# A Mamba layer's prologue: x and the gate in one tile with one Silu, the convolution's bias added at the PSUM read

## The chip, the cores and the metric

The kernel runs on one core of a Trainium2 chip. A core has a matrix engine (TensorE, PE in the profile; its weight loads are PEld), VectorE (DVE), ScalarE (ACT), GpSimd (POOL), and SyncE (SP), which here issues the DMAs. They work in parallel, each through its own list of instructions in a fixed order, and wait for one another by semaphores. The metric is the device time of one execution in microseconds (us).

## The reference

Eight layers follow one another on an activation of 8 sequences of 256 positions and 128 channels. The change is in the seventh, a pair of Mamba scans (one forward, one on the reversed sequence) between layernorms. One scan computes:

```python
xz = x @ W_in.T
xp, z = jnp.split(xz, 2, axis=-1)
xc = conv_general_dilated(xp, conv_w, ..., feature_group_count=E)   # 4 taps, causal
xc = _silu(xc + conv_b)
x_dbl = xc @ W_xp.T
dt_lo, Bm, Cm = (x_dbl[..., :R], x_dbl[..., R:R + N], x_dbl[..., R + N:])
dt = softplus(dt_lo @ W_dt.T + dt_b)
A = -jnp.exp(A_log)
def step(h, inp):                         # one position
    dA = jnp.exp(dtt[:, :, None] * A)
    h = dA * h + (dtt * xt)[:, :, None] * Bt[:, None, :]
    y = jnp.einsum('ben,bn->be', h, Ct)
y = ys + xc * Dp
y = y * _silu(z)
return y @ W_out.T
```

E is 256 channels, N is 64 states, R is 8. What matters here: x passes through a convolution, a bias and a Silu and then feeds everything that follows; the gate z passes through a Silu too, but is used only at the very end.

## The kernel before

The first six layers are interleaved by a planner of their own and end before the part that matters. The Mamba layer (`l3_attn`, from line 1838) works in eight units. A unit is two sequences (512 positions) in one direction: unit u has the pair u // 2, forward for even u and reversed for odd u. Channels lie on the partitions, so x, the gate and dt are tiles of 128 partitions by 2 by 512.

Each unit has three parts.

`prologue` (lines 1902 to 1991) makes what the scan needs. For an even unit it first normalizes x (two runs of `norm_steps` and two products on POOL). It transposes x, and copies it to `xT` (L1921). For each of two channel blocks and two sequences, four matmuls (L1929) make the convolution in PSUM, and ScalarE copies 128x256 of it to `xc` (L1931). Two matmuls (L1936) make the gate, copied to `sz` (L1938). Then come the Silus on ScalarE: two of 128x512 with the convolution's bias on `xc` (L1941), one of 128x1024 on `sz` (L1942). From `xc`, L1947 and L1950 make C, dt's low-rank part and B, copied at L1953 and L1954 and sent by SP to DRAM (`cd`) and turned (`Bt`). L1962 makes dt's argument; softplus is made of ScalarE's Abs (L1965), Exp (L1967) and four Squares (L1972) with VectorE's L1966, L1974 and L1975. POOL makes `dtx` (L1978), PE transposes it, ScalarE copies it to `dtxT` (L1990).

The loop runs 64 steps a unit, one for each state n. `start` (L2047) has SP fetch C's row to all partitions (`Cs`), ScalarE make dA by two Exps of 128x512 (L2058), and for even n scale `dtxT` by B four times (`sT`, L2055). `inputs` fills the PSUM tile `ps_h` by transposes of `sT` for even n (L2073), or by 64x64 matmuls with `dB` for odd n (L2071; `dB` is made on POOL at L2045). `scan` runs VectorE's scan over 1024 elements (L2079) and the product with C (L2081) on POOL, for one n of sixteen on VectorE. `add` transposes that into the PSUM accumulator `ps_y` (L2091).

`epilogue` (lines 1993 to 2038) turns `ps_y` back, adds xc times D on VectorE (L2006), multiplies by `sz` on POOL (L2008), projects (L2014), and after each odd unit adds both directions, normalizes twice and adds to the residual (L2022 to L2038).

The order of the work is written by hand: prologue and epilogue are generators, and each step of the loop advances each by one `yield`. The prologue of unit u + 1 starts at step 6 of unit u and has to end by step 60; the epilogue of unit u - 1 runs in the first steps of unit u. Prologue 0 runs alone ahead of the loop. After that a scheduler puts each engine's instructions into their final order, by when it takes their inputs to be ready, so the order in the trace isn't always the order of the source: the first of L1941's two Silus runs as soon as its half of `xc` is there, before the other half is copied.

The names to know: the PSUM tiles of the prologue and the epilogue (`ps_a`) and of the loop (`ps_h`) share one ring of three buffers. `dA`, `sT` and `h` have three buffers each, `xc`, `sz`, `dt`, `dtxT` two. Silu and Exp live in different activation tables, so ScalarE loads a table (ACT_TABLE_LOAD, put down to the line of the instruction that needs it) when it goes from one to the other; copies, Identity, Abs and Square run without one here.

Of the kernel before, what the change touches and what calls it, by code (L numbers as in the profile page):

```python
# [8 lines left out]
F32 = mybir.dt.float32  # L9
BF16 = mybir.dt.bfloat16  # L10
I32 = mybir.dt.int32
AF = mybir.ActivationFunctionType
# [4 lines left out]
P = 128  # L17
NB = 8
L = 256
# [247 lines left out]
def over(ap, n, axis):  # L267

    a = ap.unsqueeze(axis)
    s = list(a.shape)  # L270
    s[axis] = n
    return a.to_broadcast(s)
# [1565 lines left out]
def l3_attn(k):  # L1838
# [13 lines left out]
    nc = k.nc  # L1852
    U = 2 * L
    N = 64
    HALF = (slice(0, 64), slice(64, 128))
    with ExitStack() as es:
        s1 = es.enter_context(k.tc.tile_pool(name="l3a_s1", bufs=1))
        s2 = es.enter_context(k.tc.tile_pool(name="l3a_s2", bufs=2))
# [5 lines left out]
        def pb(name="ps_a"):  # L1864
            return psum.tile([P, 2, U], F32, name=name, tag="b")
# [25 lines left out]
        def by_seq(t):  # L1891
            return t.rearrange("p (b t) -> p b t", t=L)

        def turned(name, src):

            t = s2.tile(list(src.shape), F32, name=name)
            for b in range(2):
                for j in range(2):
                    nc.sync.dma_start(out=t[HALF[b], j::2], in_=src[HALF[j], 2 * b:2 * b + 2])
            return t  # L1900

        def prologue(u, o):
            g, m = divmod(u, 2)
            w = k.l3a[m]
            if m == 0:
                xs = xns[g] = s2.tile([P, 4, D], F32, name="xn")
                yield from k.norm_steps(xs, k.x[:, 4 * g:4 * g + 4, :], 4)
                yield from k.norm_steps(xs, xs, 4)
                nc.gpsimd.tensor_tensor(xs, xs, over(k.l3a_ln[:, 0, :], 4, 1), ALU.mult)
                nc.gpsimd.tensor_tensor(xs, xs, over(k.l3a_ln[:, 1, :], 4, 1), ALU.add)  # L1910
                yield
            xT, CL = xTs[u % 2], CLs[u % 2]
            ps = pb()
            for j in range(4):
                d = slice(j * P, (j + 1) * P)
                if m == 0:
                    nc.tensor.transpose(ps[:, 0, d], xns[g][:, j, :], k.ident)
                else:
                    nc.tensor.matmul(ps[:, 0, d], xns[g][:, j ^ 1, :], k.flip, start=True, stop=True)
            yield  # L1920
            nc.scalar.copy(xT[:, :, 3:3 + L], by_seq(ps[:, 0, :]))  # L1921
            yield

            xc, sz = s2.tile([P, 2, U], F32, name="xc"), s2.tile([P, 2, U], F32, name="sz")
            for ec in range(2):
                for b in range(2):
                    ps = pb()
                    for tap in range(4):
                        nc.tensor.matmul(ps[:, 0, 0:L], w["wk"][:, tap, ec * P:(ec + 1) * P], xT[:, b, tap:tap + L], start=tap == 0, stop=tap == 3)  # L1929
                    yield  # L1930
                    nc.scalar.copy(xc[:, ec, b * L:(b + 1) * L], ps[:, 0, 0:L])  # L1931
                    yield
                    yield
            for ec in range(2):
                ps = pb()
                nc.tensor.matmul(ps[:, 0, :], w["win"][:, 256 + ec * P:256 + (ec + 1) * P], xT[:, :, 3:3 + L], start=True, stop=True)  # L1936
                yield
                nc.scalar.copy(sz[:, ec, :], ps[:, 0, :])  # L1938
            yield
            for ec in range(2):  # L1940
                nc.scalar.activation(xc[:, ec, :], xc[:, ec, :], AF.Silu, bias=w["cols"][:, ec, 0:1])  # L1941
            nc.scalar.activation(sz, sz, AF.Silu)  # L1942
            yield

            ps = pb()
            for ec in range(2):
                nc.tensor.matmul(ps[0:72, 0, :], w["wxp"][:, ec, 64:136], xc[:, ec, :], start=ec == 0, stop=ec == 1)  # L1947
            for j in range(4):
                for ec in range(2):
                    nc.tensor.matmul(ps[:, 1, j * 64:(j + 1) * 64], xc[:, ec, j * P:(j + 1) * P], w["wxp"][:, ec, 0:64], start=ec == 0, stop=ec == 1)  # L1950
            yield
            B = s2.tile([P, 4, N], F32, name="B")
            nc.scalar.copy(CL[0:72, :], ps[0:72, 0, :])  # L1953
            nc.scalar.copy(B.rearrange("p j n -> p (j n)"), ps[:, 1, 0:256])  # L1954
            cd = dram.tile([N, U], F32, name="cd")
            nc.sync.dma_start(out=cd, in_=CL[0:64, :])
            Bt = turned("Bt", B)
            yield

            ps = pb()  # L1960
            for ec in range(2):
                nc.tensor.matmul(ps[:, ec, :], w["wdt"][64:73, ec * P:(ec + 1) * P], CL[64:73, :], start=True, stop=True)  # L1962
            un, zr = s2.tile([P, 2, U], F32, name="sp_u"), s1.tile([P, 2, U], F32, name="sp_z")
            yield
            nc.scalar.activation(un, ps, AF.Abs)  # L1965
            nc.vector.tensor_scalar(zr, ps, 0.0, None, ALU.max)  # L1966
            nc.scalar.activation(un, un, AF.Exp, scale=-1.0)  # L1967
            yield
            dt = s2.tile([P, 2, U], F32, name="dt")
            for j, (_, b) in enumerate(SP_FACTORS):  # L1970
                ps = pb()
                nc.scalar.activation(ps, un, AF.Square, bias=sp[:, j:j + 1])  # L1972
                yield
                nc.vector.scalar_tensor_tensor(dt, ps, b, dt if j else un, ALU.add, ALU.mult)  # L1974
            nc.vector.scalar_tensor_tensor(dt, dt, SP_LEAD, zr, ALU.mult, ALU.add)  # L1975
            yield
            dtx = s1.tile([P, 2, U], F32, name="dtx")
            nc.gpsimd.tensor_tensor(dtx, dt, xc, ALU.mult)  # L1978

            nc.gpsimd.memset(dt.rearrange("p e (b t) -> p e b t", t=L)[:, :, :, 0:1], 1e23)  # L1980
            yield
            yield
            dtxT = s2.tile([P, 4, 2, P], F32, name="dtxT")
            ps = pb()
            for j in range(4):
                for ec in range(2):
                    n = 2 * j + ec
                    nc.tensor.transpose(ps[:, n // 4, n % 4 * P:(n % 4 + 1) * P], dtx[:, ec, j * P:(j + 1) * P], k.ident)
            yield
            nc.scalar.copy(dtxT.rearrange("p (a j) e c -> p a (j e c)", a=2), ps)  # L1990
            o.update(xc=xc, sz=sz, cd=cd, dt=dt, dtxT=dtxT, dtxTt=turned("dtxTt", dtxT), B=B, Bt=Bt)
# [106 lines left out]
        for _ in prologue(0, made[0]):  # L2098
            pass
# [4 lines left out]
        for i in range(units * N + 4):  # L2104
            u, n = divmod(i, N)
            if n == N - 4:
                for _ in ahead:
                    pass
            if i + 3 < units * N:
                pre(made[(i + 3) // N], (i + 3) % N)  # L2110
            v, c = divmod(i - 1, N)
            if 1 <= i <= units * N:
                inputs(made[v], sts[i - 1], c)
            if i < units * N:
                sts[i] = start(made[u], k.l3a[u % 2], n)
                if n == 6 and u + 1 < units:
                    ahead = prologue(u + 1, made[u + 1])
            if 1 <= i <= units * N:
                scan(sts[i - 1], c)
            if i >= 4:  # L2120
                v, c = divmod(i - 4, N)
                add(made[v], sts.pop(i - 4), c)
                if c == N - 1:
                    for _ in behind:
                        pass
                    behind = epilogue(v, made[v])
            next(behind, None)
            next(ahead, None)
# [115 lines left out]
```

## Time and profile before

| what | value |
|---|---|
| time, median of 3 runs | 4469.94 us (4467.84 to 4470.97) |
| the profiled execution: time, span | 4469.94 us, 4468.1 us |
| granted TensorE clock | 0.922 of full speed |
| busy over the span: PE, DVE, ACT, POOL | 82%, 67%, 58%, 61% |
| prologue 0 | about 2886 to 2931 us |
| loop of the Mamba layer, first to last scan | 2937 to 4380 us |
| last layer | to 4468 us |

The whole span's shares say little of the Mamba loop, which takes a third of the time. There all engines are much busier: from 2930 to 4110 us POOL is busy for 1058.87 of 1180 us, ACT for 1019.72, DVE for 1000.43 and PE for 980.42. The chain that the page follows back from the end covers only the last layer. So the loop has to be read from stretches of it and from what each engine waited for. A line of the groups gives busy time in all and the mean of one instruction in ns, then the engine's idle time just before them and what ended it. A line of the stretches gives busy us and number of instructions for each engine.

### The profile page before, as it was taken

The page shows a single profiled execution, that of the slowest core. Times are in us where ns is not written, and L with a number is a line of the kernel's source. Part 1 is how long each engine was busy: PE and PEld are TensorE (multiplying, and loading weights), DVE is VectorE, ACT ScalarE, POOL GpSimd, SP SyncE. Part 2 cuts the span into 40 slices and gives each one's busy share as a digit, 9 for nine tenths or more (in the row PEclk, how much of TensorE's full clock was granted, in tenths as well). Part 3 has the DMA queues.
Part 4 walks back from the last instruction along what each step waited for, and adds up shares of the span by engine and source line. Part 5 has one row for each costly group of instructions (what it writes and reads, how often), then busy time and mean ns, then how long its engine had stood idle before and what let it go on. Part 6 is the DMA issues. An engine that isn't in the chain of part 4 may idle for free. (4 is left out here: it accounts for less than half of the span.)

```text
span 4468.1 us, 125288 instructions
## 1 busy us (share of the span) xinstructions
PE 3674.6 (82%) x55265; PEld 2890.7 (65%) x55265; DVE 2972.4 (67%) x4237; ACT 2583.0 (58%) x4536; POOL 2722.2 (61%) x2023
## 2 busy tenths in 40 slices
PE   6887887888778888889988887678887987888886
PEld 4776776766666655555555555467776876777774
DVE  6566565666555555644374457669888987987995
ACT  4444444434444454445554434388978888898883
POOL 5556656555664534532133243569988987988993
PEclk8998998989899999999999799889989999999997
DMA  1000000000000100000000000023333332332330
GB/s 54 3 2 2 3 2 2 3 2 8 2 2 17 35 1 7 6 23 20 1 1 1 6 1 1 10 84 105 99 90 94 107 98 82 106 101 87 106 110 29
DMA packets 98678, 168.90 MB, mean 38 GB/s; under 512 B 16699, under 2 KB 26582, under 8 KB 98006
## 3 DMA queue, kind: packets, MB, share of 16 engines
q1 hardware_dynamic: 98134, 160.89, 12.0%
q8 instruction: 434, 7.11, 0.6%
q14 instruction: 110, 0.90, 0.1%
HBM read 153.51 MB, written 2.10 MB: 35 GB/s over the span
## 5 line engine op out<-in xcount | busy, mean ns | idle before, releaser
L2081 POOL TENSOR_TENSOR hc<-h,Cs 128x1024 f32<-128x1024 f32 x480 | 1127.7, 2377 | 123.1 <-DVE h L2079 114.6
L2079 DVE TENSOR_TENSOR_SCAN h<-dA,ps_h 128x1024 f32<-128x1024 f32 x480 | 1069.7, 2271 | 122.6 <-PE ps_h L2073 38.9
L2058 ACT ACTIVATE dA<-dt,A 128x512 f32<-128x512 f32 x1024 | 684.6, 714 | 176.4 <-DVE h L2079 151.1
L2091 PE MATMUL ps_y<-w_c_ident,hc 128*128 128x128 f32 x4096 | 569.5, 284 | 131.9 <-POOL hc L2081 103.2
L2091 PEld LDWEIGHTS ps_y<-w_c_ident,hc 128*128 128x128 f32 x4096 | 462.5, 144 | 185.3 <-POOL hc L2081 175.9
L2055 ACT ACTIVATE sT<-dtxT,B 128x256 f32<-128x256 f32 x1024 | 451.3, 495 | 4.3 <-PE ps_h L2073 4.3
L580 DVE SCALAR_TENSOR_TENSOR acc<-ps,w_l0a_conv,acc 128x254 f32<-128x254 f32 (+2 forms) x768 | 313.9, 473 | 56.2 <-ACT acc L574 55.9
L2071 PE MATMUL ps_h<-dB,dtxTt 64*64 64x64 f32 x16384 | 305.6, 225 | 44.8 <-DVE h L2079 34.3
L2071 PEld LDWEIGHTS ps_h<-dB,dtxTt 64*64 64x64 f32 x16384 | 270.1, 138 | 99.1 <-DVE h L2079 46.1
L2073 PE MATMUL ps_h<-w_c_ident,sT 128*128 128x128 f32 x2048 | 280.2, 282 | 61.3 <-DVE h L2079 35.8
L2073 PEld LDWEIGHTS ps_h<-w_c_ident,sT 128*128 128x128 f32 x2048 | 241.5, 146 | 79.0 <-DVE h L2079 32.9
L790 PE MATMUL ps<-Z,XY 64*64 64x64 f32 x4608 | 192.2, 242 | 86.4 <-DVE Z L774 80.4
L349 ACT COPY XY<-ps 128x1024 f32<-128x1024 f32 (+1 forms) x128 | 120.5, 945 | 238.6 <-PE ps L797 229.0
L732 POOL TENSOR_TENSOR Ps<-M,w_c_levels 128x512 f32<-128x512 f32 x192 | 241.1, 1272 | 24.5 <-DVE M L706 24.0
L790 PEld LDWEIGHTS ps<-Z,XY 64*64 64x64 f32 x4608 | 159.8, 152 | 107.7 <-DVE Z L774 69.6
L220 POOL TENSOR_SCALAR ln_rs<-ln_mv 128x4 f32<-128x4 f32 (+1 forms) x84 | 20.2, 242 | 285.7 <-DVE ln_mv L218 275.9
L797 PE MATMUL ps<-XY,Z 64*64 64x64 f32 x5120 | 191.3, 240 | 0.5 <-issue 0.5
L771 PE MATMUL ps<-XY,Ps 64*64 64x64 f32 x5120 | 119.7, 236 | 80.9 <-ACT XY L349 29.1
L797 PEld LDWEIGHTS ps<-XY,Z 64*64 64x64 f32 x5120 | 168.0, 152 | 0.8 <-issue 0.6
L771 PEld LDWEIGHTS ps<-XY,Ps 64*64 64x64 f32 x5120 | 101.6, 146 | 102.9 <-issue 56.3
L774 DVE TENSOR_TENSOR Z<-ps,w_c_ident 128x512 f32<-128x512 f32 x160 | 107.7, 684 | 84.2 <-PE ps L771 83.6
L341 PE MATMUL ps<-ident 128*128 128x512 bf16 x401 | 111.0, 428 | 61.5 <-DVE qn L1067 19.3
(459 smaller groups left out, 8649.4 us busy)
## 6 DMA issues: line engine op xcount, KB each, us to landing
Cs<-cd SPq DMA_DIRECT2D x512, 256.0 KB, 3.2
dtxTt<-dtxT SPq DMA_DIRECT2D x32, 128.0 KB, 3.8
wk<-in_l0a_w SPq DMA_DIRECT2D x8, 256.0 KB, 6.2
w_h<-in_l1f_h SPq DMA_DIRECT2D x4, 512.0 KB, 3.9
w_l2a<-in_l2a_w SPq DMA_DIRECT2D x3, 512.0 KB, 4.0
w_l0a_wg<-in_l0a_wg SPq DMA_DIRECT2D x1, 1024.0 KB
w_qk<-in_l0f_wqkv SPq DMA_DIRECT2D x2, 512.0 KB, 3.6
cv<-in_l3a_m_conv SPq DMA_DIRECT2D x2, 512.0 KB, 5.0
```

Of the source, the lines that this page charges most:

```text
L580: nc.vector.scalar_tensor_tensor(acc[:, n, s:L], p4[:, n, 0:L - s], conv[:, h2, 4 * j + n, 3 - s:4 - s], acc[:, n, s:L], ALU.mult, ALU.add,)
L732: nc.gpsimd.tensor_tensor(t, M[:, :, 0:64], over(k.l0a_levels[:, n, :], 8, 1), ALU.mult)
L771: nc.tensor.matmul(ps[to, a, at(j)], Ps[own, h, :], XY[own, t, at(i)], start=True, stop=True)
L790: nc.tensor.matmul(ps[own, a, at(j)], XY[rows, t, at(i)], Z[rows, za, at(zj)], start=True, stop=True)
L797: nc.tensor.matmul(ps[to, a, at(4 + j)], Z[rows, za, at(zj)], XY[rows, t, at(i)], start=True, stop=True)
L2055: nc.scalar.mul(st["s"][:, j], o["dtxT"][:, j], o["B"][:, j, n:n + 1])
L2058: nc.scalar.activation(dA[:, :, ec, :], by_seq(o["dt"][:, ec, :]), AF.Exp, scale=w["A"][:, ec, n:n + 1])
L2071: nc.tensor.matmul(ps[q, b, ec, j * 64:(j + 1) * 64], o["dtxTt"][rows, j, ec, q], dB[rows, j, :], start=True, stop=True)
L2073: nc.tensor.transpose(ps[:, j // 2, ec, j % 2 * P:(j % 2 + 1) * P], st["s"][:, j, ec, :], k.ident)
L2079: nc.vector.tensor_tensor_scan(h.rearrange(flat), st["dA"].rearrange(flat), st["in"].rearrange(flat), 0.0, ALU.mult, ALU.add)
L2081: (nc.vector if on_v else nc.gpsimd).tensor_tensor(st["hc"], h, over(by_seq(st["C"]), 2, 2), ALU.mult)
L2091: nc.tensor.matmul(o["py"][:, 2 * b + j, ec, :], st["hc"][:, b, ec, j * P:(j + 1) * P], k.ident, start=first, stop=n == N - 1, is_transpos ...
```

## The change

x's convolution and the gate now lie in one tile `xz` of 128 by 4 by 512; `xc` and `sz` are views of its halves. The convolution's bias is added when its PSUM is read, by an Identity with a bias column in place of the copy. One Silu of 128x2048 takes the place of the three.

```diff
-            xc, sz = s2.tile([P, 2, U], F32, name="xc"), s2.tile([P, 2, U], F32, name="sz")
+            xz = s2.tile([P, 4, U], F32, name="xz")
+            xc, sz = xz[:, 0:2, :], xz[:, 2:4, :]
             for ec in range(2):
                 for b in range(2):
...
-                    nc.scalar.copy(xc[:, ec, b * L:(b + 1) * L], ps[:, 0, 0:L])
+                    nc.scalar.activation(xc[:, ec, b * L:(b + 1) * L], ps[:, 0, 0:L], AF.Identity, bias=w["cols"][:, ec, 0:1])
...
-            for ec in range(2):
-                nc.scalar.activation(xc[:, ec, :], xc[:, ec, :], AF.Silu, bias=w["cols"][:, ec, 0:1])
-            nc.scalar.activation(sz, sz, AF.Silu)
+            nc.scalar.activation(xz, xz, AF.Silu)
             yield
```

## The prediction

> **What bounds the kernel now.** I read the page's costliest groups first, then the busy time by stretches, then ScalarE's instructions by form, then the timelines of single engines in one prologue. From the page, two engines carry the Mamba loop almost evenly:
>
> ```profile
> L2081 POOL TENSOR_TENSOR hc<-h,Cs 128x1024 f32<-128x1024 f32 x480 | 1127.7, 2377 | 123.1 <-DVE h L2079 114.6
> L2079 DVE TENSOR_TENSOR_SCAN h<-dA,ps_h 128x1024 f32<-128x1024 f32 x480 | 1069.7, 2271 | 122.6 <-PE ps_h L2073 38.9
> ```
>
> POOL's product at 2.38 us a step is the longest, DVE's scan at 2.27 us is close behind. POOL's 123 us of idle time nearly all ends with a scan, so where POOL is late it is because DVE was. Which engine is full where is seen in stretches of the loop (an ordinary one last):
>
> ```profile
> core 0: us, PE busy (x) PEld busy (x) DVE busy (x) ACT busy (x) POOL busy (x), PEclk, DMA share, GB/s
> 2968.00:3018.00 50.00, 45.04 (x762) 38.15 (x760) 39.78 (x20) 49.75 (x85) 41.99 (x21) 0.97 0.31 100
> 3178.00:3227.00 49.00, 43.20 (x761) 36.68 (x759) 37.29 (x18) 48.38 (x83) 40.79 (x20) 1.00 0.33 104
> 3347.00:3384.00 37.00, 31.91 (x545) 25.48 (x543) 26.71 (x22) 34.49 (x64) 30.25 (x17) 0.95 0.31 91
> ...
> 3067.00:3106.00 39.00, 32.92 (x704) 28.93 (x704) 36.84 (x17) 34.02 (x64) 38.82 (x20) 1.00 0.36 109
> ```
>
> In the ordinary stretch POOL is full (38.82 of 39 us). In the first three, while the next unit's prologue runs, ScalarE is full (49.75 of 50, 48.38 of 49) and POOL and DVE lose 7 to 12 us each. So for some 50 us of each unit ScalarE is the bound. What it does there besides the loop's own work:
>
> ```profile
> L2058 ACT ACT_TABLE_LOAD x21 | 26.9, 1283 | 0.2
> L1941 ACT ACT_TABLE_LOAD x15 | 19.2, 1283 | 0.3
> L1941 ACT ACTIVATE xc<-xc,w_l3a_m_cols 128x512 f32<-128x512 f32 x16 | 11.6, 724 | 0.2
> L1931 ACT COPY xc<-ps_a 128x256 f32<-128x256 f32 x32 | 11.4, 355 | 5.9 <-PE ps_a L1929 5.8
> ...
> L1942 ACT ACT_TABLE_LOAD x7 | 9.0, 1283 | 0.1
> L1942 ACT ACTIVATE sz<-sz 128x1024 f32<-128x1024 f32 x8 | 8.5, 1058 | 0.1
> ```
>
> 22 loads stand ahead of a Silu and 21 ahead of the next dA: three Silus a unit run at three different times, each between Exps. One such excursion in ScalarE's timeline, and what DVE waited for in the same prologue (unit 2's); columns are start, duration, what ran, and in brackets the idle time before it and what ended it:
>
> ```profile
> 3195.62 1.28 ACT L1941 ACT_TABLE_LOAD   x1
> 3196.91 0.72 ACT L1941 ACTIVATE xc<-xc,w_l3a_m_cols 128x512 f32<-128x512 f32 x1
> 3197.66 1.28 ACT L2058 ACT_TABLE_LOAD   x1
> 3198.95 1.34 ACT L2058 ACTIVATE dA<-dt,A 128x512 f32<-128x512 f32 x2
> ```
>
> ```profile
> 3205.07 6.64 DVE L2079 TENSOR_TENSOR_SCAN h<-dA,ps_h 128x1024 f32<-128x1024 f32 x3 [2.14 <-PE ps_h L2073]
> 3214.38 4.46 DVE L2079 TENSOR_TENSOR_SCAN h<-dA,ps_h 128x1024 f32<-128x1024 f32 x2 [2.66 <-ACT dA L2058]
> 3224.11 1.23 DVE L1966 TENSOR_SCALAR sp_z<-ps_a 128x1024 f32<-128x1024 f32 x1 [5.26 <-ACT sp_u L1965]
> ```
>
> The first of these waits is ScalarE's too: the matmul it names (L2073) sat 1.48 us for the copy of sz (L1938), which held one of three PSUM buffers. With 0.94 us more at 3186.25 DVE lost 11.0 us in this prologue behind ScalarE.
>
> **What the Trainium skill says.** "ScalarE: Activation LUTs", section "What ACT_TABLE_LOAD costs", prices a load at about 1283 ns and the drain beside it at about 1380 ns more. The trace agrees on the load (1283) and shows no drain here: the excursion above runs from 3195.62 to 3198.95, 3.33 us, and 1.28 + 0.72 + 1.28 is 3.28. The same page, section "Table sets: the hidden batching unit", asks for calls to be batched by set; the 43 loads above are what it costs not to. The first section also gives an ACTIVATE as a fixed part and 0.833 ns an element; from this trace's Silus of 128x1024 at 1058 ns, 128x2048 is then an estimated 1058 + 853 = 1911 ns. "PSUM — Partial Sum Buffer", section "Engine vs sequencer instructions", says that ScalarE's, VectorE's and GpSimd's queues are strict FIFO, which is why work behind a load waits for it.
>
> **The change part by part.**
>
> *Table loads and Silus, prologues 1 to 7.* Gone: two excursions of 3.33 us (L1941) and one of 3.65 (3208.14 to 3211.79, L1942). Added: one of 1.28 + 1.91 + 1.28 + 0.03 = 4.50 us. That is 2 x 3.33 + 3.65 - 4.50 = 5.81 us less on ScalarE.
>
> *Bias in the convolution's copies.* Four copies of 355 ns become Identity with a bias column. The nearest row is L574, an ACTIVATE of 128x256 out of PSUM with a column operand, 474 ns in ScalarE's groups by form. So + 0.12 each, 0.48 a prologue; bounds 0 and 4 x 0.14 (against sT's 495 at L2055). Net per prologue: 5.81 - 0.48 = 5.33 us; all seven, 37.3.
>
> *How much of it comes back as time.* There are three kinds of prologue. In those of units 1, 2, 4 and 6 ScalarE has no slack from the first excursion to past the last, so the 5.33 us lie on what sets the pace; a few stalls are not ScalarE's (PE takes 0.8 to 1.5 us for each convolution between two ps_h), and the order of work on each engine is fixed, so I take 80%: 4 x 4.26 = 17.0. In those of units 3, 5 and 7 the loop also carries a layernorm in the epilogue of the unit before (L2026 to L2038): at the first excursion (3325.80) DVE then waits 4.44 us for POOL's L2033, so that excursion is hidden. ScalarE is full only from about 3347; inside it lie one L1941 excursion, the L1942 one and one copy: 3.33 + 3.65 - 4.50 - 0.12 = 2.36, at 80% 1.9, three times 5.7. After these waits go, DVE's softplus (L1966 to L1975, some 7 us of its own beside the scans) is late next.
>
> *Prologue 0.* It runs alone ahead of the loop, and here the change costs. Today xc's Silu ends when sz's copies begin, and PE starts L1947 at 2910.79; sz's own Silu is hidden beside PE:
>
> ```profile
> 2909.67 0.72 ACT L1941 ACTIVATE xc<-xc,w_l3a_m_cols 128x512 f32<-128x512 f32 x1
> 2910.30 1.27 ACT L1938 COPY sz<-ps_a 128x512 f32<-128x512 f32 x2
> 2911.61 1.06 ACT L1942 ACTIVATE sz<-sz 128x1024 f32<-128x1024 f32 x1
> ```
>
> Afterwards x waits for sz: copies to 2911.6, a load to 2912.9 (today's load sits in idle time at 2906.20), 1.91 us of Silu to 2914.8. L1947 starts 4.0 us later, and everything behind it is one chain (CL, softplus, POOL's dtx, the first dA at 2930.81; SP's store of cd and the Bt transfers move with it). Bounds: 2.7 if the load stays in idle time, 4.0 if not; I take 4.0.
>
> *Edits with no price.* The tile is as large as the two were, two buffers as before. It comes free only after POOL's L2008, not DVE's L2006: for the tightest unit L2008 ends at 3303.40 and the first convolution copy into that buffer is at 3311.41, 8 us later; if that cover went, ScalarE would stand for POOL's queue, at most one hc, 2.4 us. xc later in the prologue delays dtxT, which has 37 us and more until its unit begins (3252.96 against yT at 3294.50). The DMAs behind the CL and B copies (one of cd, four of Bt) come at most as late as these.
>
> *A wait that is added.* L1947 now waits for the gate as well, and behind it in PE's order stand ps_h and ps_y of the next steps. If ScalarE gained nothing, in unit 2's prologue the Silu would end at 3208.14 + 1.28 + 1.91 = 3211.33 where L1947 now starts at 3209.51: 1.8 us. With ScalarE 6.6 us earlier (two excursions) it is nothing; between 0 and 1.8, and I take it within the 20% left out.
>
> *The sum.* -17.0 - 5.7 + 4.0 = -18.7. The profiled execution took 4469.94 us (span 4468.1), the same as the median: 4451.
>
> **The rivals.**
>
> *All of it comes back.* The loop has 11.0 us of DVE waits behind ScalarE in unit 2's prologue, twice what is saved, so the whole 5.33 could return in each of seven: -37.3 + 4.0 = -33, 4437. For: 48.38 us busy of 49. Against: the hidden excursion in units 3, 5, 7.
>
> *Nothing comes back.* dA and sT have three buffers each, so ScalarE runs up to two steps ahead; the two early excursions (3.3 us each) might be paid out of that lead, DVE and the three PSUM buffers being the real pace. Then only prologue 0 counts: 4474. Against: the lead was gone at 3214.38, where DVE waited 2.66 us for dA.
>
> *Slower.* As before, and the one excursion, 0.85 us longer than the L1942 one, comes where PE stands for it: 1.8 us at L1947 and 0.85 of dA, 2.7 us a prologue, x 7 = 18.6, + 4.0: 4492. It decides (4479 and above) from a net loss of (8.9 - 4.0) / 7 = 0.7 us a prologue. For: L1947 starts only 0.1 to 2 us after sz's Silu today. Against: removing 6.7 us of ScalarE's work ahead of it must then be worth nothing.
>
> **How the numbers follow.** The working forecast, 4451 (4441 to 4461 by itself: 55% to 100% returned), gets 0.55; all back, 4437, 0.20; nothing back, 4474, 0.12; slower, 4492, 0.13. A change under 0.2% (8.9 us) can't be told from none. Faster by more: nearly all of the first and the second, 0.73; slower 0.13; the rest, 0.14, is the same. The range leaves out the slower case and reaches through the others: 4433 to 4477.
>
> **What would show it.** Right: about 15 loads in the loop's lines (7 or 8 ahead of a Silu, 7 ahead of dA) in place of 43; one Silu of about 1.9 us; DVE's waits for ScalarE (sp_z 15.8 us today, dA 17.3) cut by half or more; POOL's idle time down by some 20 us; the first dA 4 us later. Wrong: ScalarE no longer full in the prologues but the same idle time at DVE and POOL, or new PE waits at L1947, or the loads not gone because the scheduler puts something else between.

## The result and the profile after

The changed kernel takes 4453.94 us (median of 7 runs, 4449.68 to 4457.70), against 4466.79 us (median of 7, 4461.53 to 4470.97) for the kernel before: a ratio of 0.9971, 95% interval 0.9960 to 0.9983, or 12.9 us less. The forecast was 18.7 us less: 4451 us, reckoned from 4469.94. The median of before over seven runs is 3.2 us lower than that, so the forecast looks nearer in the time (2.9 us off) than it is in the difference (5.8 us off).

The profiled execution took 4451.59 us (span 4449.7). Its span is 18.4 us shorter than that of before, but 7.6 us of this lie ahead of the changed code: the first xT copy (L1921) starts at 2891.78 us in place of 2899.34. The instructions ahead of it are the same, and over the thirteen profiles of this study that time lies anywhere from 2889.5 to 2903.2 us. So in what follows the Mamba layer is read by itself, from its own instructions in each trace: *prologue 0* from the first xT copy to the first scan, the *loop* from there to the last unit's yT copy, and a unit from one yT copy to the next.

| us | prologue 0 | units 0, 1, 3, 5 | units 2, 4, 6 | unit 7 | loop |
|---|---|---|---|---|---|
| before | 38.08 | 707.15 | 585.93 | 155.56 | 1448.64 |
| changed | 44.94 | 698.10 | 578.79 | 154.11 | 1431.00 |
| changed, again | 47.03 | 695.96 | 580.48 | 155.68 | 1432.12 |

Units 0, 1, 3 and 5 are those in which the prologues of 1, 2, 4 and 6 run; units 2, 4 and 6 carry those of 3, 5 and 7; unit 7 carries none. The loop got 17.6 us shorter and prologue 0 6.9 us longer. The two profiles of the changed kernel differ by 1.6 to 2.1 us in each column of a part and by 1 us over the loop.

One stretch repeats much better: from a unit's first scan to its 46th, behind all the prologue's Silus. In units 1, 3 and 5 it takes 126.05 to 126.08 us before and 123.48 to 123.49 after; the six profiles of kernels with the changed loop give 123.45 to 123.53. So there the change is worth 2.6 us a prologue. From the 46th scan to the last, executions of the same loop come out up to 1.4 us apart.

ScalarE's groups by form, in the Mamba layer of the changed kernel (busy us and mean ns):

```profile
L1941 ACT ACTIVATE xz<-xz 128x2048 f32<-128x2048 f32 x8 | 15.3, 1915 | 0.1
L1932 ACT ACTIVATE xz<-ps_a,w_l3a_m_cols 128x256 f32<-128x256 f32 x32 | 14.6, 458 | 8.2 <-PE ps_a L1930 8.2
L1941 ACT ACT_TABLE_LOAD x8 | 10.3, 1283 | 0.1
...
L2057 ACT ACT_TABLE_LOAD x7 | 9.0, 1283 | 0.1
```

Fifteen loads are left of 43 (the one ahead of prologue 0's softplus, there before and after, isn't counted). The long Silu takes 1915 ns, the copy with a bias 458 ns. What DVE waited for in the same stretch (engine, line, whom it waited for; total us, times, longest):

```profile
DVE sp_z L1965 <- ACT sp_u L1964: 11.4, 3, 3.8
...
DVE h L2078 <- ACT dA L2057: 7.0, 4, 2.6
```

These two were 15.8 and 17.3 us. POOL's idle time ahead of its product fell from 123.1 to 104.6 us:

```profile
L2080 POOL TENSOR_TENSOR hc<-h,Cs 128x1024 f32<-128x1024 f32 x480 | 1127.5, 2380 | 104.6 <-DVE h L2078 90.8
```

Unit 2's prologue shows both what was gained and what took its place. DVE's timeline after the change:

```profile
3200.12 6.64 DVE L2078 TENSOR_TENSOR_SCAN h<-dA,ps_h 128x1024 f32<-128x1024 f32 x3 [0.44 <-ACT sT L2054]
3210.00 4.46 DVE L2078 TENSOR_TENSOR_SCAN h<-dA,ps_h 128x1024 f32<-128x1024 f32 x2 [3.24 <-PE ps_h L2070]
3218.26 1.22 DVE L1965 TENSOR_SCALAR sp_z<-ps_a 128x1024 f32<-128x1024 f32 x1 [3.79 <-ACT sp_u L1964]
```

The waits at these three places were 2.14, 2.66 and 5.26 us. The first has gone, the third is 1.5 us shorter. The middle one is longer and has changed hands: it was a wait for dA, and is now one for a ps_h. TensorE's timeline ahead of it:

```profile
3205.08 1.94 PE L1946 MATMUL ps_a<-xz,w_l3a_m_wxp 128*72 128x512 f32 x4 [0.36 <-ACT xz L1941]
3206.85 1.90 PE L1949 MATMUL ps_a<-w_l3a_m_wxp,xz 128*128 128x64 f32 x16
3208.68 1.16 PE L2070 MATMUL ps_h<-dB,dtxTt 64*64 64x64 f32 x64
```

The ps_h that DVE wants stands behind L1946 and L1949, which run as one piece of 3.6 us. Before L1946, TensorE stood only 0.36 us for the Silu.

Prologue 0 on TensorE, first two lines of before, then the same stretch after the change:

```profile
2910.79 1.88 PE L1947 MATMUL ps_a<-xc,w_l3a_m_wxp 128*72 128x512 f32 x4
...
2915.07 1.98 PE L1962 MATMUL ps_a<-CL,w_l3a_m_wdt 9*128 9x512 f32 x4 [0.67 <-ACT CL L1953]
```

```profile
2901.55 1.88 PE L1937 MATMUL ps_a<-xT,w_l3a_m_win 128*128 128x512 f32 x4
2907.32 3.44 PE L1946 MATMUL ps_a<-xz,w_l3a_m_wxp 128*72 128x512 f32 x4 [3.90 <-ACT xz L1941]
2910.60 1.90 PE L1949 MATMUL ps_a<-w_l3a_m_wxp,xz 128*128 128x64 f32 x16
2913.16 3.19 PE L1961 MATMUL ps_a<-CL,w_l3a_m_wdt 9*128 9x512 f32 x4 [0.67 <-ACT CL L1952]
```

The wait of 3.90 us is the one that was foreseen. But L1946 then takes 3.44 us where the same work took 1.88, and L1961 3.19 where it took 1.98.

### The profile page after: what moved, and what is told of

Read it like the earlier page. It is cut to its first block, busy times and chain, and to the rows that moved or that the text cites. A ratio compares the mean times of both kernels' runs of the same rounds, so it can differ in the third digit from the quotient of the medians.

```text
span 4449.7 us, 125255 instructions
## 1 busy us (share of the span) xinstructions
PE 3669.0 (82%) x55265; PEld 2885.0 (65%) x55265; DVE 2972.4 (67%) x4237; ACT 2550.4 (57%) x4492; POOL 2721.7 (61%) x2023
## 5 line engine op out<-in xcount | busy, mean ns | idle before, releaser
L2080 POOL TENSOR_TENSOR hc<-h,Cs 128x1024 f32<-128x1024 f32 x480 | 1127.5, 2380 | 104.6 <-DVE h L2078 90.8
```

What stands on the lines that cost most here:

```text
L2080: (nc.vector if on_v else nc.gpsimd).tensor_tensor(st["hc"], h, over(by_seq(st["C"]), 2, 2), ALU.mult)
```

## The experiments

All are edits of the changed kernel, unless another is named; line numbers shift by a few from one to the next. Where a version ran only once, its single time is not told: it varies by more than the effects do, with the time ahead of the Mamba layer. Prologue 0 and the loop are read from its trace.

**One Silu taken apart into three.**

```diff
-            nc.scalar.activation(xz, xz, AF.Silu)
+            for ec in range(2):
+                nc.scalar.activation(xc[:, ec, :], xc[:, ec, :], AF.Silu)
+            nc.scalar.activation(sz, sz, AF.Silu)
```

> The changed kernel with its one Silu taken apart again into three (x's two halves, then the gate), the bias still added where PSUM is read. Main theory (the gain in the loop is the table loads that are no longer made, the bias edit costs nearly nothing): 43 loads again, the loop from the first scan to the last yT as long as before, 1448.6 us, within 3 us (1451 if the four slower copies count in full, 0.48 us a prologue); prologue 0, from the first xT copy to the first scan, 38.1 to 38.6 us. Rival (moving the bias into the copies frees something by itself): the loop stays near the changed kernel's 1431 us.

Measured: loop 1448.06 us, prologue 0 37.79 us. Both are those of the kernel before, so the gain in the loop and the loss in prologue 0 come from joining the Silus, and the bias at the PSUM read gains nothing (up to the 46th scan of units 1, 3 and 5 this version takes 126.12 to 126.20 us, some 0.1 us more than before).

**Two Silus: x, then the gate.**

```diff
-            nc.scalar.activation(xz, xz, AF.Silu)
+            nc.scalar.activation(xc, xc, AF.Silu)
+            nc.scalar.activation(sz, sz, AF.Silu)
```

> x's Silu (128x1024) and the gate's (128x1024) apart: two excursions of about 3.65 us each in a prologue, and L1946 doesn't wait for the gate. If the saved excursions come back half, as in the change (2.5 us a prologue of 5.3 saved): one excursion of 3.3 us less than before and the bias, so the loop some 8 to 10 us shorter than before, 1439 to 1441 us. If the other half of the gain was lost to L1946 waiting for the one long Silu (the rival), this version gets it back: the loop at 1431 us or below although it has one excursion more. Prologue 0 at 38 to 39 us in both, since x's Silu no longer waits for the gate.

Measured: loop 1439.40 us, prologue 0 39.99 us. With three, two and one Silu the loop takes 1448.1, 1439.4 and 1431.0 us: some 8.5 us for each, 1.2 us a prologue. That the steps are even holds for the sum alone: up to the 46th scan of units 1, 3 and 5 the three versions take about 126.2, 125.4 and 123.5 us, so joining x's two Silus brings 0.7 us there and joining the gate's 1.9 us. L1946 waiting for the gate cost nothing that this version got back. Prologue 0 came out 1 to 2 us over the expectation, which the next run shows too.

**Prologue 0 with x's Silu ahead of the gate's.**

```diff
-            nc.scalar.activation(xz, xz, AF.Silu)
+            for part in ((xc, sz) if u == 0 else (xz,)):
+                nc.scalar.activation(part, part, AF.Silu)
```

> One Silu in the loop as in the change, but in prologue 0 x's Silu first and the gate's after it (same table, no load between). Theory: the change lost 6.9 us in prologue 0, 4.0 by the wait and 2.8 because TensorE, idle for 3.9 us, came back slow (L1946 3.44 us in place of 1.88, L1961 3.19 in place of 1.98). Without the wait both go: prologue 0 at 38 to 39 us, L1946 at 1.9, L1961 at 2.0, the loop at 1431 us as in the change, the time 6 to 7 us below the changed kernel, about 4447. Rival (the slow matmuls come from reading the joined tile, not from the idle time): only 4 us come back, prologue 0 at 41 us, L1946 still at 3.4.

Measured: 4452.10 us (median of 13 runs, 4443.04 to 4459.26), ratio to before 0.9972 (0.9963 to 0.9980); prologue 0 40.00 us, loop 1431.94. Neither expectation: the slow matmuls mostly went (L1947, in its lines, takes 1.94 us), but L1962 took 2.78 us, and TensorE still stood 1.21 us for x's Silu. The time, on another chip, can't be told from the changed kernel's.

**Matmuls in the gap of prologue 0.**

```diff
             nc.scalar.activation(xz, xz, AF.Silu)
+            if u == 0:
+                ps = pb()
+                for j in range(9):
+                    nc.tensor.matmul(ps[:, 0, :], w["win"][:, 0:P], xT[:, :, 3:3 + L], start=True, stop=True)
             yield
```

> The changed kernel with nine unused matmuls of 128x512 in prologue 0 between the gate's and L1946, so that TensorE is busy while ScalarE loads its table and runs the long Silu. They compute nothing that is used. If idle time makes the following matmuls slow: L1946 at 1.9 us in place of 3.44 and L1961 nearer to 2.0 than to 3.2, prologue 0 at 42 us in place of 44.9. If not, both stay as in the change and prologue 0 is at 45 us.

Measured: prologue 0 45.81 us, loop 1430.01. TensorE's timeline of this run (L1945 are the added ones):

```profile
2907.04 7.89 PE L1945 MATMUL ps_a<-xT,w_l3a_m_win 128*128 128x512 f32 x18
2914.77 1.88 PE L1950 MATMUL ps_a<-xz,w_l3a_m_wxp 128*72 128x512 f32 x4
2916.48 1.89 PE L1953 MATMUL ps_a<-w_l3a_m_wxp,xz 128*128 128x64 f32 x16
2919.05 1.98 PE L1965 MATMUL ps_a<-CL,w_l3a_m_wdt 9*128 9x512 f32 x4 [0.67 <-ACT CL L1956]
```

The added matmuls were twice as long as reckoned (each stands as two instructions in the trace) and outlasted the Silu by some 3.6 us, so prologue 0 as a whole got no shorter. But the matmuls behind them are back at 1.88 and 1.98 us. The granted clock says the same. First the changed kernel at L1946, then this run (columns: stretch, length, busy us and number of instructions of PE, PEld, DVE, ACT and POOL, then the clock, the DMA share and GB/s):

```profile
2907.00:2911.00 4.00, 3.68 (x9) 1.54 (x9) 0.00 (x0) 0.27 (x1) 0.00 (x0) 0.58 0.00 0
```

```profile
2914.00:2921.00 7.00, 6.33 (x27) 3.28 (x25) 0.00 (x0) 0.85 (x2) 0.00 (x0) 1.00 0.09 20
```

So the idle time makes the matmuls behind it slow, not the joined tile. The Trainium skill has this in "TensorE: Matmul & The Clock Gate", section "What's actually happening": TensorE's clock falls to half after an idle window of about 3.4 us. The 3.90 us here agree; the 1.21 us of the run before this one, with the dip behind them, are less than that window.

**Prologue 0 as before, the loop as changed.**

```diff
-            nc.scalar.activation(xz, xz, AF.Silu)
+            for part in ((xc[:, 0, :], xc[:, 1, :], sz) if u == 0 else (xz,)):
+                nc.scalar.activation(part, part, AF.Silu)
```

> One Silu in the loop as in the change, but in prologue 0 three Silus as before (x's halves, then the gate: one table, one load). Theory: TensorE then never stands for the Silu, so prologue 0 takes 37.8 to 38.1 us as in the kernel before and in the run with three Silus, the loop 1431 us as in the change: 7 us less than the change. Rival (part of prologue 0's loss comes from the bias at the PSUM read): prologue 0 stays at 39 us or above.

Measured: 4443.99 us (median of 5, 4437.98 to 4451.81), ratio to before 0.9952 (0.9937 to 0.9966); prologue 0 38.07 us, loop 1430.92 us. This is the forecast of the theory, and its median lies below both kernels'.

**The changed kernel on the same chip.** No edit.

> The changed kernel itself, on the same chip as the version above and in as many rounds: prologue 0 at 44.9 us, the loop at 1430 to 1432 us, and the time some 7 us above that version, if the time ahead of the Mamba layer, which varied from 2892 to 2903 us between executions of kernels that have the same instructions there, does not cover it.

Measured: 4453.52 us (median of 6, 4449.78 to 4460.23), ratio to the same runs of before 0.9971 (0.9958 to 0.9983), 9.5 us above the version with prologue 0 as before. Prologue 0 took 47.03 us here: the clock stayed at half for longer (L1949 also took 3.52 us). So its loss is 7 to 9 us; in the three runs below whose prologue 0 is the changed kernel's it took 44.90, 44.89 and 47.02 us.

**The burst of L1946 and L1949 split** (on the version with prologue 0 as before; L1949's loop moves one step of the main loop later).

```diff
                 nc.tensor.matmul(ps[0:72, 0, :], w["wxp"][:, ec, 64:136], xc[:, ec, :], start=ec == 0, stop=ec == 1)
+            yield
             for j in range(4):
```

> The version with prologue 0 as before, and L1946's four passes and L1949's sixteen a step of the loop apart, so that a ps_h comes between them. After the change DVE waits 3.2 us in unit 2's prologue for a ps_h that stands behind this burst of 3.6 us on TensorE, where it waited 2.7 us for dA before. If the burst took over the wait that the shorter ScalarE work set free: that wait falls below 1.5 us and the loop gets 1 to 2 us a prologue shorter, 1417 to 1424 us. Rival (ScalarE's one excursion of 4.5 us is still what DVE waits for): DVE waits for dA instead, and the loop stays within 3 us of 1431.

Measured: loop 1428.19 us. In unit 2's prologue the wait of 3.2 us has gone, and so has the one for sp_z, but smaller ones stand there instead: 1.68 us for POOL's product, 1.32 and 1.52 for ps_h, 1.74 for a Square. The burst was where the wait ended, not all of what caused it: neither theory's number, and 2.7 us in the loop are near what two profiles of one kernel differ by. Up to the 46th scan of units 1, 3 and 5 this version is 1.6 to 1.8 us ahead of the changed kernel, so the burst does cost something there, but from there to the last scan it loses 0.8 to 1.4 us of this again.

**Four buffers of dA** (on the version with prologue 0 as before).

```diff
-            dA = st["dA"] = s3.tile([P, 2, 2, L], F32, name="dA")
+            dA = st["dA"] = s3.tile([P, 2, 2, L], F32, name="dA", bufs=4)
```

> The version with prologue 0 as before, and four buffers of dA in place of three, so that ScalarE may run a step further ahead of DVE. Theory (an excursion is paid partly out of ScalarE's lead over DVE, which is why each that went gave back only 1.2 us of its 3.3): with a longer lead the one that is left costs less too, up to 1.2 us a prologue, the loop at 1423 to 1429 us, and DVE's waits for dA (7.0 us) go to nearly nothing. Rival (the lead is not limited by dA's buffers but by what else ScalarE's fixed order waits for, or DVE waits for others): within 2 us of 1431.

Measured: loop 1431.00 us, DVE's waits for dA 7.0 us, as with three. ScalarE's pauses ahead of the excursion stayed where they were (0.76, 0.73, 0.78 us), so it did not run further ahead at all, and whether a longer lead would help was not tested.

**An extra excursion, early.**

```diff
                     nc.scalar.activation(xc[:, ec, b * L:(b + 1) * L], ps[:, 0, 0:L], AF.Identity, bias=w["cols"][:, ec, 0:1])
+                    if u and ec == 0 and b == 1:
+                        nc.scalar.activation(tiny, xc[:, 0, U - 1:U], AF.Silu)
```

> The changed kernel with one unused Silu of 128x1 a prologue (units 1 to 7) after the second convolution copy, where the first of the old Silus stood: two loads and some 0.2 us more on ScalarE, 2.8 us. If an excursion costs about the same wherever it stands (1.2 us, as taking them out one by one gave): the loop at 1439 us. If ScalarE's pauses there cover it (in unit 2's prologue it waits for DVE for 3.6 us in all after the change): within 2 us of 1431. If it is paid in full: 1431 + 7 x 2.8 = 1450 us.

Measured: loop 1441.66 us, but not evenly. Units 0, 1, 3 and 5 took 698.41 us, 0.3 us more than in the change in all four together, and up to the 46th scan units 1, 3 and 5 took 123.46 to 123.52 us, as without it. Units 2, 4 and 6 took 587.59, 8.8 us more. ScalarE's pauses that cover it in unit 1 are these, from the changed kernel, all behind the second convolution copy (3175.85):

```profile
3179.90 1.33 ACT L2057 ACTIVATE dA<-dt,A 128x512 f32<-128x512 f32 x2 [0.76 <-DVE h L2078]
...
3185.30 1.33 ACT L2057 ACTIVATE dA<-dt,A 128x512 f32<-128x512 f32 x2 [0.74 <-DVE h L2078]
...
3193.12 1.34 ACT L2057 ACTIVATE dA<-dt,A 128x512 f32<-128x512 f32 x2 [0.16 <-DVE h L2078]
3195.30 1.33 ACT L2057 ACTIVATE dA<-dt,A 128x512 f32<-128x512 f32 x2 [0.84 <-DVE h L2078]
```

With the early excursion 0.37 us is left of these 2.5 us. In the kernel before none of them is there, only one pause just ahead of the first excursion (3179.49):

```profile
3173.53 1.33 ACT L2058 ACTIVATE dA<-dt,A 128x512 f32<-128x512 f32 x2 [1.24 <-DVE h L2079]
```

It is there in all three (1.14 us in the change, 1.12 here): ScalarE stood waiting for DVE when the excursion came. DVE's wait behind the excursion is 0.94 us in all three as well, for dA in the kernel before and here, for a ps_h in the change, so the excursion added nothing to it.

In unit 2 the excursion stands in the middle of the epilogue's layernorm, between the first and the other three of its four Identities, and DVE waits for what POOL makes of them (ScalarE and DVE of this run; the same wait is 4.43 us in the change):

```profile
3315.89 0.49 ACT L227 ACTIVATE x<-x,ln_mv,ln_rs 128x128 f32<-128x128 f32 x1 [3.12 <-DVE ln_mv L224]
3316.40 1.28 ACT L1935 ACT_TABLE_LOAD   x1
```

```profile
3326.62 0.49 DVE L217 BATCH_NORM_STATS2 ln_st<-x 128x6 f32<-128x128 f32 x2 [6.39 <-POOL x L2035]
```

In the kernel before, the first Silu of unit 2's loop came behind these four, so the 8.8 us are the price of this place, not of the old one.

**An extra excursion, late.** The same with `ec == 1`, reading `xc[:, 1, U - 1:U]`.

> The same after the fourth convolution copy, where the second of the old Silus stood, shortly before the gate's copies. Same cost everywhere: 1439 us. If the early one is covered and this one is what was paid before, since it makes the gate's copies late and these hold PSUM: 1431 + 17 (all that the change gained in the loop), 1448 us, or at least twice what the early one adds.

Measured: loop 1438.52 us. Units 0, 1, 3 and 5 took 703.57 us, 5.5 more than in the change (2.1, 1.8, 0.1 and 1.6); units 2, 4 and 6 took 580.85, 2.1 more. Up to the 46th scan units 1, 3 and 5 took 124.99 to 125.01 us, 1.5 more each. In the four units with the saturated prologue the late excursion is paid by half and the early one not at all.

**No table change in the loop.**

```diff
-            nc.scalar.activation(xz, xz, AF.Silu)
+            nc.scalar.activation(xz, xz, AF.Silu if u == 0 else AF.Identity)
```

> The changed kernel with Identity in place of the one Silu in the prologues of units 1 to 7: the Silu is left out of the computation there, the 128x2048 pass stays, and so no table is loaded in the loop. What the last two loads (2.57 us) still cost: if excursions go on costing 1.2 us each, the loop at 1422 us; if the wait behind them has passed to TensorE's burst of L1946 and L1949, as the trace after the change has it in unit 2's prologue, within 3 us of 1431; if they are paid in full, 1413 us.

Measured: loop 1421.92 us, 9.1 us less, 1.3 us a prologue: the first of the three numbers. By parts it isn't that case, and that the sum fits it is chance. Units 0, 1, 3 and 5 took 688.34 us, 9.8 less, 2.4 a prologue and so nearly the full 2.57 us of the two loads; up to the 46th scan of units 1, 3 and 5 it is 1.65 us each (121.80 to 121.84). Units 2, 4 and 6 took 577.94 us and unit 7 155.63, which can't be told from the change. So the last two loads are paid in great part in the saturated prologues, although TensorE's burst stands behind them.

## Why the prediction came out as it did

The direction, the place and the mechanism were right: fewer table loads on ScalarE shorten the loop, and joining the Silus lengthens prologue 0. The time lies within the range and within the working forecast's own. In part this is luck: two terms of the sum are off, and the base moved by 3.2 us. (The forecast's own 4441 to 4461 isn't 55% to 100% of the 28.4 us that it counts as on the path; with + 4.0 these give 4446 to 4458.)

*The loads and the Silus on ScalarE* (5.33 us less a prologue): right to the instruction. 43 loads became 15, the Silu was put at 1911 ns and took 1915, the copy with bias at 474 and took 458.

*The signs.* The loads and the Silu came as listed, and POOL's idle time fell by 18.5 us of "some 20". DVE's waits for ScalarE (sp_z and dA) fell from 33.1 to 18.4 us, by 44%, a little less than the half that was asked for.

*Units 0, 1, 3 and 5* (17.0 us, 80% of what ScalarE saves): 9.0 us came back (707.15 to 698.10). The step that failed is the reading that ScalarE has no slack "from the first excursion to past the last". It was busy for 48.38 of 49 us, but it had stood waiting for DVE just ahead of that stretch, and in it it was working off the 3.3 us that it had just lost. Without them it pauses for DVE, 2.5 us in all behind that place in unit 2's prologue, and an excursion put back there costs 0.3 us over four units. Only the later ones were on the path. Each step from three excursions to none takes 2.7 to 2.8 us off ScalarE; up to the 46th scan of units 1, 3 and 5 the first step gave back 0.7 us, the second 1.9 and the third, beyond the change, 1.65.

*Units 2, 4 and 6* (5.7 us): 7.1 us came back. As a sum this is near. The reading that the first excursion is hidden there holds at its place: DVE's wait for POOL's L2033 is 4.44 us with it and 4.43 us without. But with two Silus these units already took 581.03 us, so most of the gain came with joining x's two. Which excursion was paid isn't settled, since the layernorm's work on DVE and POOL stands in another order there once ScalarE is free earlier, and no run separates the two.

*Unit 7*, which has no prologue, is 1.5 us shorter in one profile of the changed kernel and 0.1 us longer in the other. The difference lies behind its last scan: from there to the last yT copy it is about 6.6 us in seven of the thirteen profiles and 8.1 to 8.3 us in six, with either in the changed kernel. So this part isn't the change's. What decides it was not tried.

*Prologue 0* (+ 4.0 us): + 6.9 and + 8.9 in two profiles. The wait is as it was worked out, 3.90 us; the term that was missing is TensorE's clock after it, 2.8 us or more. Leaving prologue 0 alone gives all of it back.

*The rivals.* "All of it comes back" fell with the free early excursion. "Nothing comes back" had the right mechanism, ScalarE paying out of slack ahead of DVE, for one of the excursions in four of seven prologues, and the wrong extent. "Slower" named L1946 waiting for the long Silu; it waited 1.6 us in all (four times, 0.5 at most; 2.3 us in the second profile), and two Silus in place of one gave nothing back.

*The sum.* -9.05 - 7.14 - 1.45 + 6.86 is -10.78 in the Mamba layer's own trace, against -18.7, and -12.9 by the medians. Half of the gain foreseen for the saturated prologues was never on the path, and the exposed prologue took 7 to 9 us of what was won.

## What to carry to other kernels

An engine that is full right after a stall may be catching up: look whether it stood waiting just ahead of the stall (here 1.24 us), and how long the engine that it feeds then waited behind it (here 0.94 us, with or without the stall), and don't count on the whole stall. When work is joined to save a fixed cost, look for the one place where it runs uncovered and where the first half was what everything waited for; there, keep it apart. And a wait that is added in front of TensorE is priced with the slow matmuls behind it, not by its own length alone.

## What the runs showed of the hardware

In prologue 0 TensorE's wait of 3.90 us was followed by a granted clock of 0.58 in place of 1.00 over the next four us in one profile; L1949 ran at full speed again (1.90 us), and L1961 didn't (3.19). In the other profile the clock stood at 0.50 for all the matmuls that followed, to 2924 us, some 11 us, the first 7 of them without a gap. In the two runs with a wait of only 1.21 us there, L1962 still took 2.78 and 2.75 us in place of 1.98, with a clock of 0.76 around it in the run with x's Silu ahead of the gate's; whether the length of that wait or the moment at which it falls decides this was not tried. A table load in this kernel costs its 1283 ns and no drain that the trace shows. Of a load, a Silu and a load on a ScalarE that is nearly always busy, the loop's time felt nothing where ScalarE had been waiting just before, and half or more further on.
